# Schedule of expert tiles, outputs and dense weights in the last steps of an adaLN block on one core

## The chip, the core and the metric

The kernel runs on one NeuronCore of a Trainium2 chip. The metric is the device time of an execution in microseconds (us). Before the change four runs took 3938.16 to 3945.1 us, with a median of 3941.16. One further execution was profiled; every duration in this document without another source comes from its trace.

The engines are named as in the profile: PE (TensorE) does the matrix products and the transposes, DVE (VectorE) and ACT (ScalarE) work on the tiles, POOL (GpSimd) does elementwise work and issues gathers and scatters by row (indirect DMAs), SP (SyncE) issues nearly all other DMAs. SP works off its list in order: while it waits for the semaphores of one DMA, nothing behind it is issued.

## The reference

The input x is (8 batches, 2048 tokens, 256 features), all in float32. With modulation vectors from a small condition, per batch:

```
h = layernorm(x) * (1 + ca) + sa
q, k = elu(h Wq)+1, elu(h Wk)+1;  v = h Wv          # 16 heads of 64
a = sigmoid(h Wa + ba + 2)                          # a decay per head and token
S_t = a_t S_(t-1) + k_t v_t^T;  z_t = a_t z_(t-1) + k_t
x = x + ga * ((q_t S_t / (q_t z_t + eps)) Wo)
h = layernorm(x) * (1 + cb) + sb
p = softmax(max(h gate_W + gate_b, 1e-4))           # 8 experts, the best 2 are kept
x = x + gb * sum over the 2 of weight * (h expert_W[e] + expert_b[e]) / 2
```

The recurrence runs along the tokens, so the batches' groups of tokens are worked off in order.

## The kernel before

**Groups and steps.** A group is 256 tokens (two chunks of 128); a batch has NG = 8 groups, so there are 64 groups. The main loop (`for n in range(-2, total + 1)`, L1135) is written by hand under a manual schedule: each engine gets its instructions in the order in which the code emits them. Step n works on four groups at once: `here` (n) does the attention of its two chunks c0 and c1, `ahead` (n+1) the projections k and q, the key sums and the denominators, `coming` (n+2) its decays, and `prev` (n-1) its second layernorm (`norm`, `modulated`), its gate (`pgate`, L628) and its routing. The generators (`kp`, `qp`, `zk`, `rt`, `da`, `dk`, `dn`, `na`) are advanced piece by piece between one another.

**Routing and units.** A unit is a stretch of groups whose tokens are sorted by expert together: in `UNITS` (L59) each of the first seven batches is one unit of 8 groups, and the last batch is one of 4 groups and one of 2. `routing` picks two experts for each token and scatters its normalised row into the lists `xrows` in DRAM (POOL, L755). After a unit's last group, `plan` (L766) makes the table of its tiles, and eight more scatters fill the lists' ends. A unit of 8, 4 or 2 groups has 39, 23 or 15 tiles of 128 rows, since each expert's list is rounded up. The last two groups (`dense_from`, L1060) are dense: all 8 experts are applied to their 256 tokens (`DenseUnit`, `DenseTile`) and weighted with `comb`; `biases` (L901) starts the sums.

**Tiles.** An `ExpertTile` has three parts. `load`: two register reads from the table, then DMAs of its rows (xg, 128 KB) and its expert's weights (we, 384 KB), both on SP. `turn`: two transposes (pxt) and two ACT operations (xgT). `apply`: four matmul records (py), an addition on DVE, and a DMA of the result (yg to yrows). At most AHEAD = 4 tiles are loaded or turned at a time, and at most two are turned. `expert_tiles(k)` (L1086) turns up to two, applies one, loads the next, k times. It is called at five places in a step (L1158, L1199, L1235, L1269, L1315); `share` (L1144 to L1152) lists how many tiles each place gets. "share[3]" below is the fourth place, between c1's scores and the denominators. Until step 56 a unit's tiles are spread evenly, some five a step. From step 57 (`late`, the last 8 steps) the shares are [3, 2, 2, 3, 2] where there are tiles. A unit whose last group is step n-1's `prev` is planned in step n and queued in step n+1, ahead of share[3].

**The burst.** Just after share[3], in each step, SP gets the broadcasts of `coming`'s decays (at), of `ahead`'s second chunk (dec, el) and of the denominators (rb); share[4] follows behind them.

**Outputs.** When all tiles of a unit are applied, a `Combine` for each of its groups waits in `waiting`. `fetch_outputs` takes one: a DMA of x from xd on SP (L979), and four gathers of rows of yrows on POOL (L990). `finish_outputs` weights and adds them (ACT, DVE, POOL) and writes the output (SP, L1011). x has one buffer (xc). Up to step 56 a step fetches one output at L1189 and finishes it at L1302. From step 57 on a step finishes and fetches at L1220 and again at L1302. In the last step (n = total) the free tiles dec, kT and qT become rooms for more outputs (`rooms`), with one of the two chunks finished on DVE. A loop after the steps (L1334) does what is left: a tile, then a finish, then a fetch.

Of the kernel before, what the change touches and what calls it, by code (L numbers as in the profile page):

```python
# [8 lines left out]
F32 = mybir.dt.float32  # L9
# [4 lines left out]
P = 128  # L14
C = 128
G = 2
GT = G * C
# [8 lines left out]
AHEAD = 4  # L26
# [4 lines left out]
def adaln_block_kernel(  # L31
# [17 lines left out]
    nc = tc.nc  # L49
    B, N, D = x.shape  # L50
# [3 lines left out]
    KD = D // P  # L54
# [1 line left out]
    NG = N // GT  # L56


    UNITS = [(b, 0, NG) for b in range(B - 1)] + [(B - 1, 0, NG - 4), (B - 1, NG - 4, NG - 2)]  # L59

    def tiles_of(unit):
        return (TOP_K * GT * (unit[2] - unit[1]) + E * (P - 1)) // P
# [559 lines left out]
    def routing(x, unit):  # L622
# [53 lines left out]
        if unit.dense:  # L676
            weigh()
            comb = unit.comb
            nc.vector.tensor_mul(comb, picks[:, :, 0, :], wide(top[:, :, 0:1]))
            nc.vector.tensor_mul(mark, picks[:, :, 1, :], wide(top[:, :, 1:2]))  # L680
            nc.vector.tensor_add(comb, comb, mark)
            yield
            unit.biases()
            yield
            return
# [205 lines left out]
    class DenseUnit:  # L891
# [29 lines left out]
        def finish(self):  # L921
            x, gt = self.x, gates_of[self.x.b]
            for ch in range(G):
                y = self.acc[:, ch, :]
                nc.vector.tensor_mul(y, y, gt[:, 1, :])
                nc.vector.tensor_add(x.xt[:, ch, :], x.xt[:, ch, :], y)
                at = x.g * GT + ch * C
                nc.sync.dma_start(out=out[x.b, at : at + C, :], in_=x.xt[:, ch, :])

    class DenseTile:  # L930


        def __init__(self, unit, e):
            self.unit, self.e, self.tag = unit, e, f"{unit.n}_{e}"

        def load(self):
            self.w = wk2.tile([P, KD + 1, D], F32, tag="we", name=f"we_{self.tag}", bufs=AHEAD)
            nc.sync.dma_start(out=self.w[:, :KD, :], in_=ew_d[self.e, :, :KD, :])

        def turn(self):  # L940
            pass
# [22 lines left out]
    class Combine:  # L964
# [5 lines left out]
        def load(self, room=None):  # L970

            u = self.unit
            self.engines = [nc.vector if room and ch else nc.gpsimd for ch in range(G)]
            if room:
                hold = wk2.tile([P, 4 * TOP_K, D], F32, tag=room, name=f"xyc_{self.tag}")
                self.x = hold[:, G * TOP_K : G * TOP_K + G, :]
            else:
                self.x = wk2.tile([P, G, D], F32, tag="xc", name=f"xc_{self.tag}", bufs=1)
            nc.sync.dma_start(  # L979
                out=self.x,  # L980
                in_=u.xd[self.g * GT : (self.g + 1) * GT, :].rearrange("(c p) d -> p c d", p=P),
            )
            self.y = {}
            for ch in range(G):
                at = (self.g - u.first) * G + ch
                for n in range(TOP_K):
                    y = hold[:, ch * TOP_K + n, :] if room else wk2.tile(
                        [P, D], F32, tag="yc", name=f"yc_{self.tag}_{ch}_{n}", bufs=4
                    )
                    nc.gpsimd.indirect_dma_start(  # L990
                        out=y,
                        out_offset=None,
                        in_=u.yrows[:, :],
                        in_offset=bass.IndirectOffsetOnAxis(ap=u.rows[:, at, n : n + 1], axis=0),
                    )
                    self.y[ch, n] = y

        def finish(self):
            u = self.unit
            gt = gates_of[u.b]  # L1000
            for ch in range(G):
                at = (self.g - u.first) * G + ch
                a, c = self.y[ch, 0], self.y[ch, 1]
                nc.scalar.activation(a, a, AF.Copy, scale=u.weights[:, at, 0:1])
                nc.vector.scalar_tensor_tensor(
                    a, c, u.weights[:, at, 1:2], a, ALU.mult, ALU.add
                )
                self.engines[ch].tensor_mul(a, a, gt[:, 1, :])
                self.engines[ch].tensor_add(self.x[:, ch, :], self.x[:, ch, :], a)
            g = self.g  # L1010
            nc.sync.dma_start(  # L1011
                out=out[u.b, g * GT : (g + 1) * GT, :].rearrange("(c p) d -> p c d", p=P),
                in_=self.x,
            )
# [12 lines left out]
    def advance(gen, k=1):  # L1027

        for _ in range(k):
            if gen is not None:  # L1030
                next(gen, None)
# [35 lines left out]
    arows = rest(norm(live[0].xt, "a", live[0].tag))  # L1067
    S = z = None
    queue, loaded, turned = [], [], []
    waiting, fetched = [], []  # L1070
    left = {}

    def load_tile():
        if queue and len(loaded) + len(turned) < AHEAD:
            t = queue.pop(0)
            t.load()
            loaded.append(t)
# [6 lines left out]
            turned.append(t)  # L1084

    def expert_tiles(k=1):  # L1086
        while queue and len(loaded) + len(turned) < AHEAD:
            load_tile()
        for _ in range(k):

            while loaded and len(turned) < 2:
                t = loaded.pop(0)
                t.turn()
                turned.append(t)
            if turned:
                now = turned.pop(0)
                now.apply()
                load_tile()
                left[now.unit.n] -= 1
                if left[now.unit.n] == 0:  # L1100
                    u = now.unit
                    waiting.extend(Combine(u, g) for g in range(u.first, u.end))
                    if u.dense:
                        u.finish()

    rooms = []

    def fetch_outputs():
        room = None
        if rooms:  # L1110
            rooms.append(rooms.pop(0))
            room = rooms[-1]
        if waiting:
            o = waiting.pop(0)
            o.load(room)
            fetched.append(o)

    def finish_outputs():
        while len(fetched) > (2 if rooms else 0):
# [14 lines left out]
    with tc.manual_schedule():  # L1134
        for n in range(-2, total + 1):  # L1135
            here, ahead, coming = live.get(n), live.get(n + 1), live.get(n + 2)
            prev = live.pop(n - 1, None)
            kp = qp = zk = rt = da = dk = dn = na = nf = c1 = None
            late = n > total - NG
            if n == total:  # L1140
                rooms.extend(["dec", "kT", "qT"])

            todo = len(queue) + len(loaded) + len(turned)
            if late and (todo or not planned):  # L1144
                share = [3, 2, 1, 3, 3] if planned else [3, 2, 2, 3, 2]
            elif planned:
                share = [0, 0, 0, 3, 3] if late else [0, 0, 0, 2, 2]
            else:
                steps = NG - (n - 1) % NG
                share = [  # L1150
                    -(-todo * (i + 1) // (5 * steps)) + (-todo * i // (5 * steps)) for i in range(5)
                ]  # L1152
            own = here.dk if here else None
            if here:
                c0.scores(0)
# [29 lines left out]
                zz, z = next(zk)  # L1185
            advance(kp)
            advance(zk)
            if not late:
                fetch_outputs()  # L1189
            if here:  # L1190
                whole_decay(here, 1)
# [4 lines left out]
            if prev:  # L1196
                prev.h2T = modulated(prev.rows, prev.b, 3, 4, f"f{prev.tag}")
            advance(kp)
            expert_tiles(share[1])  # L1199
            if prev:  # L1200
                if n - 1 == dense_from:

                    sums = wk2.tile([P, NP, GT], F32, tag="at", name="sums", bufs=1)
                    nc.sync.dma_start(out=sums[:E, 2 * G, :], in_=expert_b)
                if n - 1 >= dense_from:
                    unit = DenseUnit(prev)
                else:
                    u = unit_of[n - 1]
                    if units[u] is None:
                        units[u] = Unit(u)  # L1210
                    unit = units[u]
                rt = routing(prev, unit)
# [4 lines left out]
            advance(own, 2)  # L1217
            if here:
                c0.project()
            if late:  # L1220
                finish_outputs()
                fetch_outputs()
            if coming:
                da = decays(coming.hT, coming.tag)
            advance(da)
# [34 lines left out]
            if prev and unit.dense:  # L1260
                queue.extend(DenseTile(unit, e) for e in range(E))
                left[unit.n] = E
            advance(dk, 2)
            if here:
                c1.scores(0)
                c1.keys()
                c1.scores(1)
# [32 lines left out]
                next(ahead.dk)  # L1300
            advance(na)
            finish_outputs()  # L1302
            if late:
                fetch_outputs()
            c0 = None
            if ahead:
                c0 = Chunk(
# [7 lines left out]
            expert_tiles(share[4])  # L1315
            if here:
                c1.project()
            if here and n < dense_from:
                u = unit_of[n]
                if units[u] is None:  # L1320
                    units[u] = Unit(u)
                nc.sync.dma_start(
                    out=units[u].xd[here.g * GT : (here.g + 1) * GT, :].rearrange(
                        "(c p) d -> p c d", p=P
                    ),
                    in_=here.xt,
                )
# [3 lines left out]
                planned = unit  # L1331
        advance(plan)

        while queue or loaded or turned:  # L1334
            expert_tiles(1)
            finish_outputs()
            fetch_outputs()
# [38 lines left out]
```

## Time and profile before

| what | value |
|---|---|
| median of the four runs | 3941.16 us |
| the profiled execution's own time | 3943.86 us |
| its span, first to last instruction | 3942.1 us |
| busy: PE, DVE, ACT, POOL | 3561.0, 2629.2, 2089.6, 1857.5 us |
| mean granted clock of PE | 0.961 |
| moved by DMA | 714.19 MB, 181 GB/s over the span |
| longest waits of PE: pxt (L868) for xg | 85.6 us, 15 times, longest 15.6 |
| longest waits of SP: led (L374) for ACT; yrows (L889) for yg on DVE | 505.8 us; 479.9 us |
| SP: xc<-xd (L979) for the output write before it | 90.8 us, 13 times, longest 14.9 |

A busy engine in the profile is one that runs an instruction; the rest of its time it waits, and the views name the instruction that ended the wait. SP's long waits are not by themselves costs: what counts is which other engine waits behind SP. The timelines list start, length, engine, line, operation, out<-in and, in square brackets, the idle time before it with its releaser.

### The profile page before, as it was taken

The page shows a single profiled execution, that of the slowest core. Times are in us where ns is not written, and L with a number is a line of the kernel's source. Part 1 is how long each engine was busy: PE and PEld are TensorE (multiplying, and loading weights), DVE is VectorE, ACT ScalarE, POOL GpSimd, SP SyncE. Part 2 cuts the span into 40 slices and gives each one's busy share as a digit, 9 for nine tenths or more (in the row PEclk, how much of TensorE's full clock was granted, in tenths as well). Part 3 has the DMA queues.
Part 4 walks back from the last instruction along what each step waited for, and adds up shares of the span by engine and source line. Part 5 has one row for each costly group of instructions (what it writes and reads, how often), then busy time and mean ns, then how long its engine had stood idle before and what let it go on. Part 6 is the DMA issues. An engine that isn't in the chain of part 4 may idle for free.

```text
span 3942.1 us, 82178 instructions
## 1 busy us (share of the span) xinstructions
PE 3561.0 (90%) x28998; PEld 2741.7 (70%) x28998; DVE 2629.2 (67%) x6380; ACT 2089.6 (53%) x5423; POOL 1857.5 (47%) x2002
## 2 busy tenths in 40 slices
PE   5999989999999999999899999999899998668775
PEld 3777767777777777777677777777677776556554
DVE  3777777777766676776776677666767667446534
ACT  3555555555555555555565555556555555445421
POOL 1444343344545454544654545454554445335444
PEclk9999999999999999999999999999999999889887
DMA  6444456665667657656666756766576676665655
GB/s 186 130 130 128 127 157 175 194 199 163 191 196 212 175 170 221 176 176 203 197 178 193 213 165 186 211 194 177 167 227 172 184 210 168 190 182 171 197 173 183
DMA packets 347596, 714.19 MB, mean 181 GB/s; under 512 B 43928, under 2 KB 211112, under 8 KB 322608
## 3 DMA queue, kind: packets, MB, share of 16 engines
q1 hardware_dynamic: 313680, 627.61, 56.6%
q0 software_dynamic: 27264, 74.49, 5.5%
q10 hardware_dynamic: 6240, 6.84, 0.6%
q8 instruction: 229, 3.75, 0.4%
q14 instruction: 183, 1.50, 0.1%
HBM read 579.38 MB, written 132.53 MB: 181 GB/s over the span
## 4 chain that ended last, share of the span: by engine, by line
PE 59%; DVE 15%; ACT 8%; issue 7%; DMA 5%; POOL 3%; SPq 1%; another core or an unknown queue 1%; DVEq 0%; ACTq 0%; POOLq 0%
PE pv L528 10%; PE pw L615 9%; PE pq L326 7%; PE pk L326 6%; PE po L565 6%; PE py L884 5%; PE sc L492 4%; PE ps L599 3%; DVE at L433 3%; PE po L548 3%; ACT dec L415 2%; PE pd L449 2%; PE pk L511 2%; DMA out_dram<-xc 2%; POOL at L1131 1%
## 5 line engine op out<-in xcount | busy, mean ns | idle before, releaser
L415 ACT ACTIVATE dec<-dec,lt 128x128 f32<-128x128 f32 x2048 | 632.1, 391 | 14.6 <-POOL dec L409 14.6
L1131 POOL TENSOR_TENSOR at<-at,qT 128x512 f32<-128x512 f32 x256 | 325.7, 1283 | 580.4 <-DVE rmark L713 404.8
L326 PE MATMUL pk<-hT_a,wk_sb 128*128 128x256 f32 x2048 | 512.4, 394 | 8.3 <-issue 7.9
L326 PE MATMUL pq<-hT_a,wq_sb 128*128 128x256 f32 x2048 | 484.8, 391 | 14.7 <-DVE kT L338 14.0
L615 PE MATMUL pw<-wo_sb,oT 128*128 128x256 f32 x2048 | 481.4, 390 | 4.9 <-DVE oT L577 4.9
L528 PE MATMUL pv<-wv_sb,hT_a 128*128 128x512 f32 x1024 | 475.9, 608 | 3.2 <-DVE yg L888 3.1
L873 ACT ACTIVATE xgT<-pxt,modT,modT 128x128 f32<-128x128 f32 x622 | 246.3, 449 | 399.7 <-PE pxt L868 369.6
L326 PEld LDWEIGHTS pq<-hT_a,wq_sb 128*128 128x128 f32 x2048 | 393.9, 195 | 78.7 <-DVE kT L338 20.5
L615 PEld LDWEIGHTS pw<-wo_sb,oT 128*128 128x128 f32 x2048 | 395.7, 196 | 60.9 <-DVE oT L577 6.1
L326 PEld LDWEIGHTS pk<-hT_a,wk_sb 128*128 128x128 f32 x2048 | 378.8, 195 | 76.8 <-issue 20.7
L884 PE MATMUL py<-we,xgT 128*128 128x256 f32 x1244 | 352.1, 409 | 61.2 <-ACT xgT L873 32.9
L409 POOL TENSOR_SCALAR_AFFINE_SELECT dec<-dec 128x2048 f32<-128x2048 f32 x128 | 256.8, 2006 | 267.0 <-DMA dec<-led 189.3
L577 DVE TENSOR_TENSOR oT<-po,rb 128x512 f32<-128x512 f32 x256 | 173.4, 690 | 283.2 <-PE po L565 127.0
L433 DVE TENSOR_TENSOR_SCAN at<-at,z,kT 128x256 f32<-128x256 f32 x448 | 358.9, 841 | 2.0
L501 DVE TENSOR_TENSOR dec<-sc,dec 128x512 f32<-128x512 f32 x512 | 326.9, 680 | 44.5 <-PE sc L492 38.7
L528 PEld LDWEIGHTS pv<-wv_sb,hT_a 128*128 128x128 f32 x1024 | 191.8, 193 | 219.6 <-issue 177.4
L620 POOL TENSOR_TENSOR xt<-xt,dx 128x256 f32<-128x256 f32 x128 | 94.8, 740 | 473.3 <-DVE dx L619 472.9
L565 PE MATMUL po<-dec,v 128*64 128x128 f32 x4096 | 271.0, 277 | 33.5 <-issue 23.1
L884 PEld LDWEIGHTS py<-we,xgT 128*128 128x128 f32 x1244 | 229.5, 202 | 102.5 <-ACT xgT L873 39.5
L492 PE MATMUL sc<-qT,kT 64*128 64x128 f32 x4096 | 298.1, 286 | 0.1
L492 PEld LDWEIGHTS sc<-qT,kT 64*128 64x128 f32 x4096 | 250.2, 188 | 63.4 <-issue 62.6
L1038 POOL TENSOR_TENSOR el<-el,qT 128x1024 f32<-128x1024 f32 x120 | 284.2, 2368 | 5.5
(199 smaller groups left out, 6065.8 us busy)
## 6 DMA issues: line engine op xcount, KB each, us to landing
dec<-led SPq DMA_DIRECT2D x128, 1024.0 KB
we<-ew_d SPq DMA_DIRECT2D x311, 384.0 KB
at<-ad SPq DMA_DIRECT2D x128, 512.0 KB
el<-led SPq DMA_DIRECT2D x256, 256.0 KB
rb<-rdd SPq DMA_DIRECT2D x128, 512.0 KB
xg<-xrows SPq DMA_DIRECT2D x311, 128.0 KB
yrows<-yg SPq DMA_DIRECT2D x311, 128.0 KB
xt<-in_L_attn_x_dram SPq DMA_DIRECT2D x64, 256.0 KB
```

The costliest lines, as they stand in the source:

```text
L326: nc.tensor.matmul(pp[:, j * GT : (j + 1) * GT], w[:, k, (jj + j) * P : (jj + j + 1) * P], hT[:, k, :], start=(k == 0), stop=(k == KD - 1),)
L409: nc.gpsimd.affine_select(out=dec, in_=dec, compare_op=ALU.is_ge, fill=1e30, base=0, pattern=[[0, H], [1, C]], channel_multiplier=-1,)
L415: nc.scalar.activation(dec[:, h, :], dec[:, h, :], AF.Exp, scale=-1.0, bias=x.lt[:, 0, ch, h : h + 1])
L433: nc.vector.tensor_tensor_scan(zz[:, j, :], at[:, j, :], kT[:, j, :], 0.0 if z is None else z[:, j : j + 1], ALU.mult, ALU.add,)
L492: nc.tensor.matmul(sc[q][:, i, :], self.kT[rows, half * 4 + i, self.tok], self.qT[rows, half * 4 + i, self.tok], start=True, stop=True,)
L501: nc.vector.tensor_mul(w4, sc[q], w4)
L528: nc.tensor.matmul(pv, self.hT[:, k, self.tok], wv_sb[:, k, i * 512 : (i + 1) * 512], start=(k == 0), stop=(k == KD - 1),)
L565: nc.tensor.matmul(po[half * DH : (half + 1) * DH, i, :], self.v[:, h * DH : (h + 1) * DH], self.dec[:, q * NP + j, :], start=(self.S is N ...
L615: nc.tensor.matmul(pw[:, :D], self.oT[:, j, :], wo_sb[:, j, :], start=(j == 0), stop=(j == NP - 1))
L884: nc.tensor.matmul(py[:, :D], self.xT[:, k, :], self.w[:, k, :], start=(k == 0), stop=(k == KD - 1))
L1038: nc.gpsimd.tensor_mul(el, el, x.qT[:, :, ch * C : (ch + 1) * C])
L1131: nc.gpsimd.tensor_mul(zz[:, part, :], zz[:, part, :], ahead.qT[:, part, :])
```

## The change

Five things are changed.

- The seventh batch becomes two units of four groups. Its tiles are 23 and 23 in place of 39, and the first half's can begin four steps earlier.
- From step 49 to step 59 a step with tiles gets the shares [2, 1, 1, 2, 2], eight a step, also in the step in which a planned unit is queued. The old late shares stay from step 60 on, and step 63 has [3, 2, 1, 0, 3].
- Steps 53 to 64 finish outputs in mid-step and at the end, and fetch two a step, at the two calls of `fetch_outputs(False)`: the gathers alone. The DMA of x is a part of its own, `load_x`, and is issued later by `fetch_x`: ahead of share[1], ahead of c1's scores, and after the steps.
- The dense tiles no longer load weights for themselves. In step 63 four DMAs put all eight experts' weights into wq_sb and wk_sb, whose last readers, the projections of the last group, are in step 62. Dense tiles don't count among the four on chip, and in the last step they are queued in turns with the other tiles.
- The dense routing has two more yields ahead of `biases`, and an output in a room is finished on DVE for both chunks.

```diff
-    UNITS = [(b, 0, NG) for b in range(B - 1)] + [(B - 1, 0, NG - 4), (B - 1, NG - 4, NG - 2)]
+    UNITS = [(b, 0, NG) for b in range(B - 2)] + [
+        (B - 2, 0, NG // 2), (B - 2, NG // 2, NG), (B - 1, 0, NG - 4), (B - 1, NG - 4, NG - 2)
+    ]
...
             nc.vector.tensor_add(comb, comb, mark)
+            yield
+            yield
             yield
             unit.biases()
...
+            part = slice(e % 4 * D, (e % 4 + 1) * D)
+            self.w = (wq_sb, wk_sb)[e // 4][:, :, part]
+
         def load(self):
-            self.w = wk2.tile([P, KD + 1, D], F32, tag="we", name=f"we_{self.tag}", bufs=AHEAD)
-            nc.sync.dma_start(out=self.w[:, :KD, :], in_=ew_d[self.e, :, :KD, :])
+            pass
...
+        def load_x(self):
+            if self.x is None:
+                self.x = wk2.tile([P, G, D], F32, tag="xc", name=f"xc_{self.tag}", bufs=1)
+            nc.sync.dma_start(
+                out=self.x,
+                in_=self.unit.xd[self.g * GT : (self.g + 1) * GT, :].rearrange(
+                    "(c p) d -> p c d", p=P
+                ),
+            )
...
     def load_tile():
-        if queue and len(loaded) + len(turned) < AHEAD:
+        if queue and (queue[0].unit.dense or on_chip() < AHEAD):
...
-    def fetch_outputs():
+    def fetch_outputs(x=True):
...
             o.load(room)
             fetched.append(o)
+            if x:
+                o.load_x()
+            else:
+                no_x.append(o)
+
+    def fetch_x():
+        while no_x:
+            no_x.pop(0).load_x()
...
-            late = n > total - NG
+            twice = n > total - NG - 4
+            late = n > total - 5
             if n == total:
                 rooms.extend(["dec", "kT", "qT"])
+
+                tiles = [t for t in loaded + queue if not t.unit.dense]
+                dense = [t for t in loaded + queue if t.unit.dense]
+                some, loaded[:], queue[:] = len(loaded), [], []
+                while tiles or dense:
+                    (loaded if some > 0 else queue).extend(tiles[:1] + dense[:1])
+                    some -= 1
+                    del tiles[:1], dense[:1]
...
             if late and (todo or not planned):
                 share = [3, 2, 1, 3, 3] if planned else [3, 2, 2, 3, 2]
+            elif planned and not todo:
+                share = [0, 0, 0, 3, 3] if late else [0, 0, 0, 2, 2]
+            elif n > total - 2 * NG:
+                share = [2, 1, 1, 2, 2]
             elif planned:
-                share = [0, 0, 0, 3, 3] if late else [0, 0, 0, 2, 2]
+                share = [0, 0, 0, 2, 2]
...
+            if n == total - 1:
+                share = [3, 2, 1, 0, 3]
...
-            if not late:
+            if not twice:
                 fetch_outputs()
...
             advance(kp)
+            fetch_x()
             expert_tiles(share[1])
...
+                if n - 1 == dense_from:
+
+                    for e in range(0, E, 4):
+                        for k in range(KD):
+                            nc.sync.dma_start(
+                                out=(wq_sb, wk_sb)[e // 4][:, k, :].rearrange(
+                                    "p (e f) -> p e f", f=D
+                                ),
+                                in_=ew_d[e : e + 4, :, k, :].rearrange("e p f -> p e f"),
+                            )
...
-            if late:
+            if twice:
                 finish_outputs()
-                fetch_outputs()
+                fetch_outputs(False)
...
             advance(dk, 2)
+            fetch_x()
             if here:
                 c1.scores(0)
...
             finish_outputs()
-            if late:
-                fetch_outputs()
...
             expert_tiles(share[4])
             if here:
                 c1.project()
+            if twice:
+                fetch_outputs(False)
...
         advance(plan)
 
+        fetch_x()
         while queue or loaded or turned:
```

More of the change, by code (lines that the diff above doesn't have):

```diff
@@ L972, in load @@
             u = self.unit
-            self.engines = [nc.vector if room and ch else nc.gpsimd for ch in range(G)]
+            self.engine = nc.vector if room else nc.gpsimd
             if room:
@@ L977, in load @@
             else:
[L978 to L982, printed above, removed]
+                self.x = None
             self.y = {}
@@ L1007, in finish @@
                 )
-                self.engines[ch].tensor_mul(a, a, gt[:, 1, :])
-                self.engines[ch].tensor_add(self.x[:, ch, :], self.x[:, ch, :], a)
+                self.engine.tensor_mul(a, a, gt[:, 1, :])
+                self.engine.tensor_add(self.x[:, ch, :], self.x[:, ch, :], a)
             g = self.g
@@ L1069, in adaln_block_kernel, with on_chip @@
     queue, loaded, turned = [], [], []
-    waiting, fetched = [], []
+    waiting, fetched, no_x = [], [], []
     left = {}
+    def on_chip():
+        return sum(not t.unit.dense for t in loaded + turned)
     def load_tile():
-        if queue and len(loaded) + len(turned) < AHEAD:
+        if queue and (queue[0].unit.dense or on_chip() < AHEAD):
             t = queue.pop(0)
@@ L1086, in expert_tiles @@
     def expert_tiles(k=1):
-        while queue and len(loaded) + len(turned) < AHEAD:
+        while queue and not queue[0].unit.dense and on_chip() < AHEAD:
+            load_tile()
+        if queue and not loaded:
             load_tile()
```

## Prediction

> **What bounds the kernel now.** I read the page from the top: which engine is busiest, and where it isn't.
>
> ```profile
> PE 3561.0 (90%) x28998; PEld 2741.7 (70%) x28998; DVE 2629.2 (67%) x6380; ACT 2089.6 (53%) x5423; POOL 1857.5 (47%) x2002
> ...
> PE   5999989999999999999899999999899998668775
> ...
> PEclk9999999999999999999999999999999999889887
> ```
>
> PE is the bound for 33 slices; in the last seven it is idle more and its granted clock falls. To see why, I cut the span by step: the gate matmuls (pgate, L628) come once a step, and "stretch n" is the time from step n's to step n+1's. From stretch 49 on they last 64.7, 57.4, 56.1, 56.8, 56.4, 59.3, 55.9, 53.6 us (49 to 56), 94.1, 88.6, 88.7, 59.9, 90.8, 77.5, 63.6 (57 to 63), and 83.3 from the last gate to the end. Three of them in the view by windows (length, then busy time of PE; at the end clock, DMA share, GB/s):
>
> ```profile
> 773.70:827.10 53.40, 52.99 (x462) 41.64 (x461) 40.52 (x94) 32.08 (x84) 21.18 (x22) 1.00 0.64 182
> ...
> 3013.60:3070.40 56.80, 54.30 (x461) 41.43 (x460) 39.62 (x97) 32.47 (x86) 28.79 (x31) 1.00 0.67 193
> ...
> 3389.80:3478.40 88.60, 66.54 (x504) 50.78 (x503) 43.21 (x105) 38.83 (x101) 35.93 (x38) 0.87 0.66 184
> ```
>
> The first has 5 expert tiles and no output, the second 5 tiles and one output, the third 12 tiles and two. The third leaves PE idle for 22 us at a clock of 0.87. The timelines of PE and of SP's queue name the place:
>
> ```profile
> 3441.24 1.03 PE L884 MATMUL py<-we,xgT 128*128 128x256 f32 x4
> 3457.30 0.66 PE L868 MATMUL pxt<-ident,xg 128*128 128x128 f32 x2 [15.03 <-DMA xg<-xrows]
> 3457.75 1.91 PE L884 MATMUL py<-we,xgT 128*128 128x256 f32 x4
> ```
>
> ```profile
> 3431.15 1.15 SPq L395 DMA_DIRECT2D at<-ad  x2
> 3432.40 0.53 SPq L405 DMA_DIRECT2D dec<-led  x1
> 3434.11 1.54 SPq L465 DMA_DIRECT2D rb<-rdd  x2
> 3435.70 1.29 SPq L395 DMA_DIRECT2D el<-led  x2
> 3437.03 0.59 SPq L1011 DMA_DIRECT2D out_dram<-xc  x1
> 3452.69 0.38 SPq L979 DMA_DIRECT2D xc<-xd  x1
> ...
> 3455.14 0.36 SPq L851 DMA_DIRECT2D xg<-xrows  x1
> ```
>
> Once a step SP issues a burst of 2.5 MB (0.5 at, 1.0 dec, 0.5 rb, 0.5 el). The output write goes in behind it, and the x load L979 waits 15.6 us for that write, because xc has one buffer. All tile loads wait behind L979, and PE waits for xg. The waits of PE from 3295 to 3795 hold 77.1 us of this.
>
> **Where tile loads fall.** Four tiles are on chip; a new one is loaded when one is applied, and a tile is turned (pxt) one tile ahead. Counting this ring through the shares, in the 12-tile steps the two refills made in share[4], behind the burst, are turned in share[0] of the next step, where the 15 us stand. With shares [1,1,1,1,1] no refill made in share[4] is needed before share[2]. With the new [2,1,1,2,2] the first refill of share[4] is turned at the second tile of share[0]. So the new steps keep one such wait, even with L979 out of the way, if the burst is still draining. Stretch 49 has two tiles each in share[3] and share[4] already and shows both times:
>
> ```profile
> 2873.24 1.12 SPq L395 DMA_DIRECT2D at<-ad  x2
> ...
> 2883.25 0.34 SPq L851 DMA_DIRECT2D xg<-xrows  x1
> ```
>
> ```profile
> 2886.78 1.03 PE L884 MATMUL py<-we,xgT 128*128 128x256 f32 x4
> 2887.65 3.60 PE L528 MATMUL pv<-wv_sb,hT_a 128*128 128x512 f32 x8
> ```
>
> A second tile of share[0] would be turned at 2887.7. In the trace's packet records the burst's last 2 KB packets (rb) move at 2888.8 and the 3 KB packets of expert weights, which follow xg in the queue, start at 2890.8; the write of the output and xg (1 KB packets) lie between and after. So xg lands at about 2891.5 to 2892.5, and PE waits 4 to 5 us. Measured from the pd matmuls, the burst ends alike in the other steps (22 to 25 us after them).
>
> **The change part by part**, against the profiled execution's own time of 3943.9 us (span 3942.1).
> - *Tiles.* Two units of 23 in place of one of 39 add 7 tiles (311 to 318). A tile is 1.15 us of PE: in share[3], pxt starts 1.14 apart (3417.36, 3418.50). By the shares, the stretches hold 6, then six times 5, 3, 11, 12, 12, 4, 11, 12, 11 and 20 (the end) tiles before, and 7, six times 8, 7, 7, 8, 8, 0, 11, 12, 8 and 23 after.
> - *Pairs.* A second tile in a share waits for its ACT turn: 0.2, 1.5 or 2.6 us in the rows (3420.66, 3433.25, 2878.79). I take 1.0 a step.
> - *The small stall.* 4.5 us, and then a slower clock: after an idle time of 3.5 us a py group took 2.07 (not 1.03) and a pq group 2.48 (not 1.89), +1.6; after the 15 us, two py and pv lost 3.5. I take 2.2, so 6.7 a step; bounds 0 (the load wins) and 18.5 (15 us and its slow clock, as before). It comes in ten stretches: 49 to 55, 57 to 59.
> - *A second output* costs 2.8, the difference of a stretch with one output and one with none (56.8 less the 53.4 to 54 of the first batch); with its finish in mid-step VectorE and PE show waits of 3.5 (3403.88), so 0 to 5.
> - *One more unit boundary*, in step 53: eight scatters on POOL (10 us, 3296 to 3306), the plan on DVE. Stretch 49, a boundary, lasts 7 us more than the next; there the tiles also start late, here 11 are left. I take 3.6, bounds 0 and 8.
> - *x loads apart.* L979 leaves the place behind the burst. In stretches 61 and 62, with shares unchanged, xg still waits for the burst: it ends at 3450, the output write at 3452.6, where xg came at 3457.3. I take 6.5 each (bounds 0 and 20).
>
> Sums. Stretch 49: +7 (tile 1.2, stall 6). 50 to 52: 3.5+1+6.7 = +11.2 each. 53: 11.2+2.8+3.6 = +17.6. 54 and 55: +14 each. 56: four tiles, an output, a pair = +8.4. Together +94.6. 57 becomes a boundary with 7 tiles, 64.7+7+2.8+3.5 (its wait for the decays was 6.0, in 49 it was 2.5) = 78: -16. 58 and 59 become 56.8+11.2+2.8 = 71: -17.6 and -17.7. From the other side: 88.6 less 15 of stall, 3.7 of slow clock and 4 tiles is 65, and with 6.7 it is 72. 60 loses 4 tiles: -4.4. 61 and 62: -13. Together -68.7. **The regular steps so lose 26 us**: the work that was late is moved, dearer, to steps in which PE had been full.
>
> **The end** pays for that. Step 63 loses a wait of 5.8 us for comb (the two yields put the bias matmuls behind other work), a wait of 5.2 for xg behind L979, and 3 tiles with their waits: 63.6 to 47, -16.6. After the last gate there were six outputs, each 6.5 us on POOL (four gathers of 1.25, two operations), and every dense tile took its turn with one:
>
> ```profile
> 3907.97 3.75 PE L948 MATMUL py_d<-we_d,hT_f 128*128 128x256 f32 x8 [4.49 <-DMA we_d<-ew_d]
> ```
>
> After, two outputs are left, and the dense weights lie in wq_sb and wk_sb since step 63 (2 MB, about 9 us of queue under work that doesn't need it). 14 dense tiles at 1.75 (seven ran in 12.25 at 3871) and 9 others at 1.15 are 35 us, biases and turns 4, and 11 from the last py_d to the end as before: 50 for 83.3, -33.3 (bounds -15 and -42).
>
> Total: +26 - 50 = -24, 3919.9 for the profiled execution; its 2.7 us over the median taken off, **3917**.
>
> [...]
>
> **Rivals.**
> 1. *The load wins.* If the burst ends earlier or share[0] comes later by 4 us, the ten stalls go: 67 less, 3850. For it: the output gathers leave the burst (0.5 MB). Against it: the packet times above.
> 2. *Slower: the small stall is not small.* Ten steps now put two tile loads ahead of the burst and more behind it. With 9 us and 3.5 of slow clock at share[0] a step costs 5.8 more: 3975. It decides from 3.2 us a step on. For it: the DMA share is 0.99 to 1.05 from 2874 to 2898 with six tiles; against it: stretch 49 had the same load.
> 3. *The end is not shorter*, since the last two groups' gathers still wait for the last tiles' writes, or x is late: 25 instead of 50 gained, 3942, no change.
> 4. *The change doesn't free the queue*: L1011 itself waits for POOL ahead of the tile loads. That takes the 13 us of stretches 61 and 62 back, 3930, inside the forecast.
>
> **Chances.** Forecast (with 4) 0.45, its own range 3890 to 3945; rival 1 0.20, rival 2 0.23, rival 3 0.12. The range leaves out half of rivals 1 and 2: 3850 to 3972. A difference under 0.2% (8 us) can't be told from none: faster is under 3933, slower over 3949. Faster 0.36+0.20+0.02, same 0.07+0.02+0.06, slower 0.02+0.21+0.04.
>
> **What would show it.** Stretches 50 to 52 near 68 us with one wait of pxt for xg of 4 to 5 us each at share[0]; 58 and 59 near 71; 61 and 62 still with a wait of some 10 us; no wait of L979's line for the write; no wait for dense weights, and 50 us after the last gate. Stretches 50 to 52 at 61 mean rival 1, at 74 rival 2; an end over 65 us means rival 3. The working is wrong if the ring is: then the waits stand at another share.

## The result and the profile after

The change makes the kernel slower. The median is 3953.86 us over 52 runs, against 3941.92 us for the kernel before over 78 runs made beside them; the ratio is 1.0035 with a 95% interval of 1.0026 to 1.0043. The profiled execution has a span of 3951.8 us, 9.7 more than the one of before.

The first view is the page of the kernel after: busy time by engine, then PE and its granted clock in 40 slices.

```profile
PE 3568.7 (90%) x29042; PEld 2753.3 (70%) x29042; DVE 2652.0 (67%) x6408; ACT 2095.5 (53%) x5437; POOL 1867.9 (47%) x2018
...
PE   5999999999999999999899999999888888878787
...
PEclk9999999999999999999999999999999989999998
```

The deep holes of the last seven slices (6 and 5) are gone. In their place the last twelve slices all stand at 7 or 8. The idle time has not been removed but spread over twice as many steps.

Cut by step as before (from gate matmul to gate matmul, which are now line L630), the stretches compare as follows; times in us.

| stretch | before | forecast | after |
|---|---|---|---|
| 49 | 64.7 | 72 | 74.2 |
| 50, 51, 52 | 57.4, 56.1, 56.8 | 68.6, 67.3, 68.0 | 68.5, 68.3, 68.6 |
| 53, 54, 55 | 56.4, 59.3, 56.0 | 74.0, 73.3, 69.9 | 75.3, 73.7, 71.5 |
| 56 | 53.6 | 62.0 | 68.8 |
| 57, 58, 59 | 94.1, 88.6, 88.7 | 78, 71, 71 | 75.8, 72.2, 73.7 |
| 60, 61, 62 | 59.9, 90.8, 77.5 | 55.5, 84.3, 71.0 | 57.0, 84.8, 72.7 |
| 63 | 63.6 | 47 | 48.8 |
| the end | 83.3 | 50 | 59.0 |

Stretches 49 to 56 cost 109 us more, 57 to 62 give 63 back, stretch 63 gives 15 and the end 24. That is 6 us more; the other 3.5 lie ahead of step 49, where the two kernels are the same.

What an eight-tile step looks like inside: the timelines of PE and of SP at the change from step 50 to 51 (start, length, engine, line, operation; in brackets the idle time before and its releaser).

```profile
2957.80 0.44 PE L872 MATMUL pxt<-ident,xg 128*128 128x128 f32 x2
2958.07 1.03 PE L888 MATMUL py<-we,xgT 128*128 128x256 f32 x4
2965.86 0.66 PE L872 MATMUL pxt<-ident,xg 128*128 128x128 f32 x2 [6.76 <-DMA xg<-xrows]
2966.31 1.91 PE L888 MATMUL py<-we,xgT 128*128 128x256 f32 x4
```

```profile
2946.53 1.12 SPq L397 DMA_DIRECT2D at<-ad  x2
2947.74 0.53 SPq L407 DMA_DIRECT2D dec<-led  x1
2948.68 1.30 SPq L467 DMA_DIRECT2D rb<-rdd  x2
2950.03 1.24 SPq L397 DMA_DIRECT2D el<-led  x2
2952.25 0.40 SPq L1023 DMA_DIRECT2D out_dram<-xc  x1
2952.75 0.41 SPq L893 DMA_DIRECT2D yrows<-yg  x1
2954.84 0.34 SPq L855 DMA_DIRECT2D xg<-xrows  x1
```

The x load no longer stands between the output write and the tile loads, and no gap between two of these lines is over 2 us. Still, xg is issued at 2954.8 and PE gets it at 2965.9, 11 us later, because the burst is in the queue ahead of it: in the packet records its last packets (4 KB each, of el) move at 2963.9, and those of xg end after them. It is the second tile of share[0] that waits. The burst is larger than the prediction says: at and rb are two DMAs of 512 KB each, so it is 3.5 MB (1.0 at, 1.0 dec, 1.0 rb, 0.5 el), and not 2.5. Over stretches 49 to 59 the view of PE's waits says:

```profile
PE pxt L872 <- DMA xg<-xrows: 61.2, 9, 8.6
PE py L888 <- ACT xgT L877: 24.9, 21, 2.6
...
PE pxt L872 <- issue: 6.6, 1, 6.6
```

With the one that is put down to "issue" (step 51 to 52, the same place) these are the ten waits of the forecast, 6.8 us each. The second line is the second tile of a share waiting for its ACT turn.

### The profile page after: what moved, and what is told of

The parts are those of the page before. It is cut to its first block, busy times and chain, and to the rows that moved or that the text cites. A ratio compares the mean times of both kernels' runs of the same rounds, so it can differ in the third digit from the quotient of the medians.

```text
span 3951.8 us, 82386 instructions
## 1 busy us (share of the span) xinstructions
PE 3568.7 (90%) x29042; PEld 2753.3 (70%) x29042; DVE 2652.0 (67%) x6408; ACT 2095.5 (53%) x5437; POOL 1867.9 (47%) x2018
## 4 chain that ended last, share of the span: by engine, by line
PE 58%; DVE 16%; issue 7%; ACT 6%; DMA 6%; POOL 4%; SPq 1%; another core or an unknown queue 0%; DVEq 0%; POOLq 0%; ACTq 0%
PE pv L530 9%; PE pw L617 8%; PE pk L328 7%; PE pq L328 7%; PE po L567 5%; PE py L888 5%; PE sc L494 3%; DMA xg<-xrows 3%; DVE at L435 3%; PE ps L601 3%; PE po L550 2%; POOL at L1156 2%; PE pd L451 2%; ACT dec L417 2%; PE pk L513 2%
## 5 line engine op out<-in xcount | busy, mean ns | idle before, releaser
L328 PE MATMUL pq<-hT_a,wq_sb 128*128 128x256 f32 x2048 | 492.7, 396 | 27.7 <-DVE kT L340 13.2
```

Of the source, the lines that this page charges most:

```text
L328: nc.tensor.matmul(pp[:, j * GT : (j + 1) * GT], w[:, k, (jj + j) * P : (jj + j + 1) * P], hT[:, k, :], start=(k == 0), stop=(k == KD - 1),)
```

## The experiments

My theory (A): the loss comes from the ten waits at the second tile of share[0], and these come from the place of that tile's load, behind the burst. The rivals: (B) the work itself costs, since it was moved into steps in which PE was full; (C) the x load that waits for the output write is the whole cause, and a queue without it has no waits; (D) it takes the load of eight tiles a step to make the wait.

The first four kernels ran on one chip beside 16 runs of the kernel before (3944.2 us). The others ran on a second chip, on which the kernel before takes 3821.5 us (11 runs) and 3820.8 us (9 runs), so ratios to the kernel before are compared, and microseconds only within a chip.

**1. Eight tiles, one of them at share[0]** (e1_rotated_share), on the changed kernel:

```diff
-                share = [2, 1, 1, 2, 2]
+                share = [1, 2, 1, 2, 2]
```

> The changed kernel with the shares [1, 2, 1, 2, 2] in place of [2, 1, 1, 2, 2]: eight tiles a step as before, but only one at share[0]. Theory A (the loss is the wait of PE for the first refill of share[4], turned at the second tile of share[0] while the burst drains): nine of the ten waits go, at about 6.9 us and 2.2 us of slow clock each, so some 80 us less than the changed kernel: about 3875 us, 1.7% under the kernel before. Theory B (the loss is the work itself, seven tiles, a boundary and second outputs put into steps in which PE was full): within 10 us of the changed kernel, 3945 to 3965 us.

Measured: 3870.75 us, ratio 0.9825 (0.9792 to 0.9858). One tile a step moved from one place to the next, and the loss of 0.35% is a gain of 1.75%. The waits of PE for xg in the last steps fall from 87.0 us to

```profile
PE pxt L872 <- DMA xg<-xrows: 32.9, 6, 12.2
```

and what is left are the stretches from 59 on and the end. Theory A holds. B as the cause of the loss does not, since the work is the same; what the moved work costs is seen in experiment 6.

**2. x apart alone** (e2_x_apart_alone), on the kernel before: `load_x`, `fetch_x` and `fetch_outputs(False)` as in the change, in the last eight steps.

```diff
-            if late:
-                fetch_outputs()
             c0 = None
...
+            if late:
+                fetch_outputs(False)
```

> The kernel before with one part of the change: in its last eight steps x is loaded apart from the gathers. Theory A (tile loads of the 12-tile steps wait for the burst, the x load only adds its last few us): the five waits shrink from 15 to about 10 us, some 30 us less than before, 3912 us. Theory C (the x load that waits for the output write is the whole cause of the waits): the five waits go with their slow clock, some 90 us less, 3850 us.

Measured: 3917.13 us, ratio 0.9930 (0.9904 to 0.9956). The five waits of 11 to 15.6 us are now 9.9, 10.3, 11.1, 12.4 and 7.4 us: they shrink by a few us and stay. Theory C falls. An in-order queue had shown the wait of L979, 15.6 us long, right ahead of the tile loads, and yet only a third of it was its own.

**3. Five tiles a step, bunched** (e3_five_tiles_bunched), on the kernel before:

```diff
+                if total - 2 * NG + 1 < n < total - NG:
+                    share = [2, 0, 0, 1, 2]
```

> The kernel before with its five tiles a step at other places in steps 50 to 55: [2, 0, 0, 1, 2] for [1, 1, 1, 1, 1]. The first refill of share[4] is then turned at the second tile of share[0]. Theory A: six new waits of pxt for xg of 4 to 7 us, with their slow clock, so 40 to 55 us more than before, 3980 to 3997 us. Theory D (it takes the load of eight tiles a step): within 8 us of the kernel before, no new waits.

Measured: 3988.49 us, ratio 1.0121 (1.0093 to 1.0148). Not a tile more than before, and 44 us are lost: six new waits of 4.6 to 7.8 us at the second tile of share[0], one of them

```profile
2961.14 0.66 PE L868 MATMUL pxt<-ident,xg 128*128 128x128 f32 x2 [7.76 <-DMA xg<-xrows]
2961.60 1.91 PE L884 MATMUL py<-we,xgT 128*128 128x256 f32 x4
```

Theory D falls: the place makes the wait, not the load.

**4. The dense weights apart, alone** (e4_dense_apart_alone), on the kernel before: `DenseTile`, `load_tile`, the four DMAs of step 63, the order in the last step, the yields and the shares of step 63 as in the change.

> The kernel before with one part of the change: the dense weights in wq_sb and wk_sb, the later biases, the other tile order in the last step and the shares of step 63; six outputs are still left for the end. If the end was bound by the outputs on POOL (6.5 us each), step 63 gives some 10 us and the end about 5: 3927 us. If it was bound by the loads of the dense weights, step 63 and the end give 35 us or more: 3907 us or less.

Measured: 3920.57 us, ratio 0.9938 (0.9918 to 0.9958). Stretch 63 falls from 63.6 to 52.5 us and the end from 83.3 to 72.7, so 11 and 11 us. The expectation of 5 for the end was too low: with weights that are there, dense tiles run on (from 3885.28 four of them in 8.34 us, where in the kernel before seven of the last ones waited 2.1 to 4.6 us for their weights). But six outputs still set most of the end.

**5. All shares rotated** (e5_all_rotated), on the changed kernel:

```diff
-                share = [3, 2, 1, 3, 3] if planned else [3, 2, 2, 3, 2]
+                share = [1, 3, 2, 3, 3] if planned else [1, 3, 3, 3, 2]
...
-                share = [2, 1, 1, 2, 2]
+                share = [1, 2, 1, 2, 2]
...
```

> The changed kernel with [1, 2, 1, 2, 2] in steps 49 to 59 and the late shares rotated too: [1, 3, 3, 3, 2] for [3, 2, 2, 3, 2], [0, 0, 0, 3, 2] for [0, 0, 0, 3, 3], [1, 3, 2, 0, 3] in step 63. Theory A: the waits that were left with the first rotation (33 us in 6 waits, and some 10 us of slow clock) go to a third: 25 to 40 us less than with the first rotation alone, about 3838 us. If a wait only moves to share[1], whose first tile then needs the load behind the burst: within 8 us of the first rotation, 3871 us.

Measured: 3722.03 us, ratio 0.9733 (0.9715 to 0.9751); 3838 of 3942 would be 0.974. Four waits for xg with 3.9 us in all are left.

**6. x apart, dense weights apart and late shares rotated, on the kernel before** (e6_parts_and_rotation_on_before): units, tiles and outputs up to step 56 as they were.

> The kernel before with x apart, the dense weights apart and the late shares rotated to [1, 3, 3, 3, 2], but its units, its five tiles a step up to step 56 and its outputs a step as they were. Theory A: x apart gave 27 us and the dense weights 24; the rotation takes the 62 us of waits for xg that x apart left to a third, and some 15 us of slow clock: 3835 us. Theory E (the eight-tile steps and the two units are needed for the gain): over 3875 us.

Measured: 3695.59 us, ratio 0.9688 (0.9667 to 0.9709), the fastest of all, and 26 us under experiment 5 on the same chip. So the two units and the eight-tile steps do not gain once the waits are gone either: they cost. The windows of stretch 51 show how (the first is experiment 5 with eight tiles, the second experiment 6 with five):

```profile
2867.84:2928.26 60.42, 56.86 (x479) 44.29 (x478) 43.63 (x99) 34.95 (x91) 28.75 (x30) 1.00 0.70 201
```

```profile
2850.85:2904.26 53.41, 52.98 (x461) 41.65 (x460) 40.41 (x96) 32.76 (x86) 27.91 (x30) 1.00 0.70 200
```

PE is busy 3.9 us more for three tiles, 1.3 each, and idle 3.1 us more, 2.5 of them since pairs of tiles wait for ACT (0.20, 1.54 and 0.74 us in experiment 5, none in experiment 6). So a moved tile costs 2.3 us in a step in which PE was full, 7.0 a step; theory B is right about that much. The small stall with its slow clock costs 8.9 a step.

**7. A ring of five** (e7_ring_of_five), on the changed kernel:

```diff
-AHEAD = 4
+AHEAD = 5
```

> The changed kernel as it is, with AHEAD = 5 in place of 4: one more tile on chip, no tile moved. Theory A: what is turned at the second tile of share[0] was then loaded ahead of the burst, so all ten small waits go, and the 12-tile steps keep theirs, one tile later: 80 to 95 us less than the changed kernel, 3865 us. If it is the place of the tiles in the step that matters, not the load: within 10 us of the changed kernel.

Measured: 3789.24 us, ratio 0.9916 (0.9902 to 0.9930): 1.2% under the changed kernel's ratio, some 45 us on this chip, not 80 to 95. The changed kernel itself was not run on this chip. The ten waits for xg are gone as expected, two of the 12-tile steps are left, but a new wait stands at the head of PE's list, and VectorE's and ACT's lists lead on to its cause:

```profile
PE po L567 <- ACT v L537: 55.7, 13, 7.6
...
PE pxt L872 <- DMA xg<-xrows: 19.7, 2, 11.2
```

```profile
ACT lny_f L276 <- DVE mv_f L272: 119.1, 16, 10.9
```

```profile
DVE yg L892 <- DMA yrows<-yg: 100.4, 15, 10.6
```

Read from the bottom: a result tile yg has three buffers, and its write to yrows lies behind the burst as well. VectorE waits for a buffer; behind it wait the statistics of the layernorm, behind these ACT's operations, behind these the copy of v, and PE. The first wait had covered a second one with the same root.

**8. The rotated kernel with one unit** (e8_rotated_one_unit): experiment 1 with `UNITS` as before.

> The rotated kernel ([1, 2, 1, 2, 2]) with the seventh batch as one unit again: 7 tiles and a boundary less (-12 us), but its 39 tiles can't begin before step 57, two more steps get 12 tiles with their waits (+25), and about seven outputs in place of two are left for the end (+20): 30 us more than the rotated kernel, 3900 us. If the split costs more than it gives: 3860 us or less.

Measured: 3772.37 us, ratio 0.9866 (0.9849 to 0.9884), between the two cases, against 0.9825 for experiment 1 on the other chip. With the intervals of both, the split of the batch gives the rotated kernel between -0.1 and 0.9%. It was not compared on one chip.

**9. A ring of five with the writes on another queue** (e9_ring_of_five_writes_apart):

```diff
-AHEAD = 4
+AHEAD = 5
...
-            nc.sync.dma_start(out=self.unit.yrows[self.i * P : (self.i + 1) * P, :], in_=y)
+            eng = nc.gpsimd if self.unit.n >= 5 else nc.sync
+            eng.dma_start(out=self.unit.yrows[self.i * P : (self.i + 1) * P, :], in_=y)
```

> The changed kernel with AHEAD = 5 and, for the tiles of the last units, the writes of the results (yg to yrows) issued by POOL on its own queue, not by SP behind the burst. In the ring of five VectorE waited 100 us for the three yg buffers, whose writes lie behind the burst, and PE then 56 us for v. If that is the second bound: these waits go and the time falls by 35 to 60 us under the ring of five (0.9916 of before), to 0.976 to 0.983 of before. If POOL's own work (a descriptor of about 1 us a tile, eight a step) takes its place, or the writes still wait for busy DMA engines: no less than 0.989.

Measured: 3737.05 us, ratio 0.9780 (0.9765 to 0.9796), 52 us under the ring of five. VectorE's wait for the buffers falls from 100.4 us to

```profile
DVE yg L892 <- DMA yrows<-yg: 14.3, 8, 5.0
```

and the wait for v has left the head of PE's list. The 1 us a tile that was expected of POOL was near what issuing a gather takes it in the kernel before (L990, 0.95 us at the median). The second bound was the writes behind the burst. The gain has two parts, which this run does not separate: the writes are in another queue, and SP's list no longer holds them up, nor they what follows them in it.

**10. x and dense weights apart, nothing else** (e11_x_and_dense_apart), on the kernel before.

> The kernel before with the two parts of the change that gained when alone, x apart (0.9930) and the dense weights apart (0.9938), and nothing else: no two units, no eight-tile steps, no second outputs before step 57, no rotation. If they add up: 0.987 of before, some 51 us less, so that the rest of the change (units, shares, outputs) costs some 63 us. If both gain by the same few waits at the end: 0.992.

Measured: 3757.13 us, ratio 0.9829 (0.9815 to 0.9844). The two parts add up, and a little more. So by the ratios, which come from two chips, the rest of the change (units, shares, more outputs) takes 2.1% back, some 80 us. That is as much as experiment 1 gains by removing most of the ten waits, which are part of this rest.

## Why the prediction was wrong

- **The mechanism** was right: the x load was not the root, the new shares keep one wait a step, in the ten stretches that were named, and the end pays. Ten of the sixteen parts came within 1.7 us. That is in part luck: in stretches 50 to 52 the waits at share[0] were 6.5 us longer in all than priced, but PE's busy time grew by 13.2 us (163.4 to 176.6) where the tiles and the slow clock had been put at 17.1. Why it grew by less no run shows.
- **The step that failed is the size of the small stall**, taken as 4.5 us; it measured 6.8 on average (3.7 to 8.6), 23 us more in ten. With 6.8 in its place the forecast's sum is 3940 us, no gain. The first row here is of the kernel before, from stretch 49, which the working used; the others are of the kernel after, in stretch 51:

```profile
2866.17 1.07 PE L449 MATMUL pd<-at,sel 128*32 128x256 f32 x16
```

```profile
3007.00 1.07 PE L451 MATMUL pd<-at,sel 128*32 128x256 f32 x16
...
3034.20 0.66 PE L872 MATMUL pxt<-ident,xg 128*128 128x128 f32 x2 [6.62 <-issue]
```

  PE stood at the second tile at 3027.6, 20.6 us after the pd matmuls; in the rows used it would have been 21.5 (2887.7). So PE came 0.9 us earlier, and the load was late besides. The working put its landing at 25.3 to 26.3 us after pd (2891.5 to 2892.5), close behind the start of the weights' packets at 24.6; PE was released at 27.2. It took the 2 KB packets of rb for the end of the burst, 22.6 us after pd; in stretch 51 they end at 23.1, but the 4 KB packets of el move until 25.1, and mostly behind them those of the output write, of yg's write and of xg, until some 26. The weights' packets start there at 25.2, before xg's have ended, so their start does not tell the landing; and the working left almost nothing for the time between the last packet and the release.
- **The rest of the miss.** The forecast for the profiled execution was 24 us less, and it took 9.7 more. Of these 33.5 us the ten stretches with a stall make up 8.7 together, since their other terms, priced too high, gave back more than half of the 23; the end makes up 9.0, stretch 56 6.8, stretches 60 to 63 5.5, and 3.5 lie ahead of step 49. So the stall takes the gain away, and the loss needs the end and stretch 56 too.
- **The slow clock** after the stall was taken as 2.2: pxt lost 0.2, py 0.9 (1.91 for 1.03) and pv 0.3 to 1.8 (3.86 to 5.37 for 3.60), 2.1 on average. That fits. At the change from step 50 to 51 the granted clock was 0.50 from 2965.86 to 2968.00 us, 0.73 in the next 4 us and 1.00 in the 4 us behind them.
- **The end**, taken as 50 us, is 59. There are two outputs instead of six and no wait for dense weights, as forecast. The loads of these weights, put at about 9 us of queue, took 7.8, from their first issue (L1250, 3845.47) to the end of POOL's wait for the last of them (L992, 3853.28). But PE is busy for 41.2 us, at a mean granted clock of 0.90, where tiles, biases and turns had been put at 39, and 7.0 us of waits between had been put at nothing: PE waited 2.4 us for xg, and the last two groups of dense matmuls were kept apart by VectorE, which now finishes both chunks of an output:

```profile
3924.30 8.26 PE L954 MATMUL py_d<-wq_sb,hT_f 128*128 128x256 f32 x32
3933.98 7.17 PE L954 MATMUL py_d<-wk_sb,hT_f 128*128 128x256 f32 x32 [1.41 <-DVE xyc L1021]
```

- **Stretch 56** was priced at 62 without a stall, and took 68.8. The views of VectorE's and PE's waits in it say:

```profile
DVE yg L892 <- DMA yrows<-yg: 6.4, 1, 6.4
```

```profile
PE po L567 <- ACT v L537: 4.0, 1, 4.0
```

  This is the second bound that experiment 7 laid bare, which was not in the working.
- **x apart** in stretches 61 and 62 (6.5 us each) measured 6.0 and 4.8. Stretches 53 to 59 without 56, in which a boundary, second outputs and pairs were added, came within 2.7 us of the forecast each; the runs don't separate these terms.
- **Rival 2** comes nearest to what happened: the small stall is not small. It asked for 3.2 us a step more. The stall brought 2.3 of them, and the end and stretch 56 more than the rest. Rivals 1, 3 and 4 did not happen: the load never won, the end is 24 us shorter, and L1023, which waited for POOL 83.4 us in all, didn't hold up a tile load in stretches 50 and 51. The chance of 0.27 for a slower kernel was low for a sum in which a landing and a chain of waits at the end had no margin.

## What to carry to other kernels

A prefetch was here not as deep as its number of buffers, but as deep as what was issued ahead of the largest transfer of its queue: with four tiles on chip PE stood still ten times, 6.8 us on average. So count for each load which burst stands before it and which instruction uses it first, and move the use, not the amount. When a wait is found behind a blocked queue, ask what the transfer would meet if the queue were free; here it met 10 us of the 15. And a ring that is made deeper can lay bare the next ring behind the same burst, as in experiment 7 (100.4 us of VectorE's waits).

## What the runs showed of the hardware

In which queue a write stood, and behind what, counted here. In experiment 9 the result writes left SP's queue for POOL's, at an unchanged DMA load (717.75 MB in both), and VectorE's wait for them fell from 100.4 to 14.3 us. The timelines of VectorE, SP and POOL show two shares in this. The 15 writes that VectorE waited for in experiment 7 had been issued 4.1 us after their tile was ready, on average, and VectorE went on 12.1 us after the issue; for the eight of experiment 9 it is 2.7 and 7.6 us. So a write was issued sooner, and was also done sooner once issued. Why the time after the issue fell too, no run shows.

The two chips differ by 3.2% on the kernel before (3944.2 and 3821.5 us). Most of that lies ahead of the stretches at issue: the gate of step 49 comes at 2835.4 us in the kernel before and at 2731.7 in experiment 10, whose code is the same up to there, 104 of the 122 us. From 600 to 2700 us PE waits 37.1 us for "issue" on the first chip, and none of these waits is listed on the second. Why is open: the kernel before was not profiled on the second one.
